# Two pools in the Mamba stage, group-norm scales made inside the attention loop, and a different order of key loads

## The chip, the cores and the metric

The kernel runs on one core of one Trainium2 chip. The metric is device time in microseconds. Before the change three runs took 4524.57, 4528.81 and 4533.37 us; their median is 4528.81 us. One further execution was profiled; its trace is the source of all timelines and rows below.

The engines are named as in the profile: PE (TensorE; PEld is its weight load), DVE (VectorE), ACT (ScalarE), POOL (GpSimd) and SP (SyncE, which issues DMAs). A queue name with a "q" (SPq) marks an instruction that issues a DMA or waits.

## The reference

Two layers, each with a group norm ahead and a residual sum behind it, on two images of 256 channels and 64 x 64 = 4096 pixels, in float32:

```
x = x + mamba_block(gn(x))        # layer norm, W_in, conv4, silu, selective scan over 4096 steps,
                                  # gate silu(z), W_out, + yn, then an MLP of 256-1024-256 with exact gelu
qkv = qkv_w @ gn(x) + qkv_b       # 8 heads of 32 channels
x = x + softmax(q^T k / sqrt(32)) @ v
gn(v): 32 groups of 8 channels, (v - mean) / sqrt(var + 1e-5)
```

## The kernel before

**Mamba stage.** `mamba_stage` walks 16 tiles of 512 columns, eight for each image. Its work is written as tasks with a cost and a due time, and `Plan.order` sorts them into one list which fixes the order of instructions on each engine. All its SBUF tiles come out of pools: weights from `l0w`, and the working tiles, as rings (`Ring`), from the pool `l0s` (`sb`): `u`, `z`, `xm`, `dt`, `b`, `c`, `h` and others of the scan, and `yn`, `hid`, `x_back` of the part behind it. A tile's tail is: output projection (L625, reads `z`), the MLP up with gelu (L429 `w`, L650 writes `hid`), the MLP down (L661), the sum (L671), the group-norm statistics (L672 into `stats1`), the store to `x_dram` (L675). The image is kept in `Scratch` in DRAM.

The Mamba stage also makes q, k and v of image 0 (`qkv`, one call per tile): the tile's x is loaded back into a `hid` tile, normalised, projected, split into a high and a low half (L714 on ACT, L718 on DVE) and stored to `qk_dram` (L723) and `v_dram`. Since `hid` is a ring of one, the last gelus have to wait for the last of these stores to land.

**Attention.** `attention_block` runs once for each image. It opens its pools in this order: `wp` (`v`, `b_qkv`, `ones`), PSUM pools, `p2` (queries, 2 buffers), `kp` (keys, 8), `ep` and `ec` (exponentials). Memory is handed out by pool, so a pool of the attention can be written only when what lay at its addresses in the stage before has been read.

For image 0 (`prepared`), `load_prepared` loads the queries of the first tile, then eight times a tile of keys and of values, all on SP. For image 1, `prepare` makes q, k and v itself: it loads `w_qkv`, makes the group-norm scales from the statistics (`group_norm_scales`, L30), and for eight tiles loads x (L984), normalises (L988), projects k and q (L998), splits and stores them (L1008 to L1011), projects v (L1021) and copies it from PSUM to SBUF (L1028, DVE). Behind each tile's projections it loads the keys of the tile before it. All of it is under `manual_schedule`, so each engine gets its instructions in the order of the code.

The loop then has 512 steps for an image (2 groups of heads x 8 query tiles x 32 key chunks). Step s does two exponentials of 128 x 1024 on ACT (L1108), the product with v for step s-1 on PE (L1129), and the logits of step s+1 on PE (four matmuls, L1095) into two of three PSUM buffers `s`. DVE and POOL sum the exponentials (L1121, L1157 to L1162). The end of a query tile (`finish`) is a generator, run a piece at a time by `Slots`: each `yield n` puts the next piece n steps later; it is started by `side.start(slot, generator)`, and `side.run()` is called once a step, between `values` and `logits`.

The scales before the change end in a square root on ACT and a reciprocal on DVE:

```
nc.scalar.activation(sd, ps2[:, 0:1], AF.Sqrt, bias=eps_t)
nc.vector.reciprocal(sc[:, 1:2], sd)
```

Of the kernel before, what the change touches and what calls it, by code (L numbers as in the profile page):

```python
# [26 lines left out]
EPS = 1e-5  # L27


def group_norm_scales(nc, small, psum, tag, stats, gmat, eps_t):  # L30


    out = []
    for k in range(stats.shape[1]):
        mv = small.tile([P, 2], F32, name="gn_mv")
        nc.vector.bn_aggr(mv, stats[:, k, :, :].rearrange("p a s -> p (a s)"))
        ps = psum.tile([P, T], F32, name="gn_mean_ps", tag=tag)
        nc.tensor.matmul(ps[:, 0:1], lhsT=gmat, rhs=mv[:, 0:1], start=True, stop=True)
        sc = small.tile([P, 2], F32, name="gn_sc", bufs=4)
        nc.vector.tensor_copy(sc[:, 0:1], ps[:, 0:1])  # L40


        d = small.tile([P, 1], F32, name="gn_d")
        nc.vector.tensor_sub(d, mv[:, 0:1], sc[:, 0:1])
        e = small.tile([P, 1], F32, name="gn_e")
        nc.vector.scalar_tensor_tensor(e, d, d, mv[:, 1:2], ALU.mult, ALU.add)
        ps2 = psum.tile([P, T], F32, name="gn_var_ps", tag=tag)
        nc.tensor.matmul(ps2[:, 0:1], lhsT=gmat, rhs=e, start=True, stop=True)
        sd = small.tile([P, 1], F32, name="gn_sd")
        nc.scalar.activation(sd, ps2[:, 0:1], AF.Sqrt, bias=eps_t)  # L50
        nc.vector.reciprocal(sc[:, 1:2], sd)
        out.append(sc)
    return out


class Slots:
# [196 lines left out]
def mamba_stage(ctx, tc, xs, stats_out, consts, w, outs, scratch):  # L253
# [43 lines left out]
    r_yn, r_u, r_z = ring("yn", 3, KC), ring("u", KD + 1), ring("z", KD)  # L297
    r_xm = Ring(sb, [P, HALO + T], "xm", 3)
    r_tmp = ring("tmp", 3, free=True)
    r_lw, r_dt = ring("lw", 2), ring("dt", 2)  # L300
    r_dtr, r_dtur = ring("dt_rep", 4, 2), ring("dtu_rep", 4, 2)
    r_b, r_c = ring("b", NQ), ring("c", NQ)
    r_da0, r_da1 = ring("da0", 3), ring("da1", 2, pool=ps)
    r_bn, r_dbu1 = ring("bn", 2, pool=ps), ring("dbu1", 3)
    r_h, r_y = ring("h", 5, 2), ring("y", 1, pool=ps)
    r_proj, r_bc = ring("proj", 2), ring("bc", 1, rows=NP)
    r_hid, r_xb = ring("hid", 1, KH), ring("x_back", 1, KC)
    r_gn = Ring(sb, [P, 8], "gn", 2)

# [595 lines left out]
        return self.x[b * KG : (b + 1) * KG].rearrange("g c t -> (g c) t")  # L905


def load_stack(nc, dst, src, which):

    src = src.rearrange("s c h t -> s c (h t)")
    dst = dst.rearrange("p h t -> p (h t)").bitcast(F32)
    for i in range(2):
        if which:
            nc.sync.dma_start(dst[2 * i * D : 2 * (i + 1) * D, :], src.rearrange("s c x -> (s c) x"))
        else:
            for j in range(2):
                nc.sync.dma_start(dst[(2 * i + j) * D : (2 * i + j + 1) * D, :], src[i])


@with_exitstack
def attention_block(ctx, tc, b, stats, consts, w, out, scratch, range_t, prepared):

# [26 lines left out]
    p2 = ctx.enter_context(tc.tile_pool(name=f"l1p2{b}", bufs=2))  # L951
# [6 lines left out]
    def load_keys(g, t):  # L958


        k = keys[g, t] = (kq if g and t == 0 else kp).tile([P, 4, T], F32R, name="k")
        load_stack(nc, k, scratch.qk[b * KG + g, 1, t], 1)

    def load_queries(i):
        if i < KG * NT:
            g, t = divmod(i, NT)
            q = queries[i] = p2.tile([P, 4, T], F32R, name="q")
            load_stack(nc, q, scratch.qk[b * KG + g, 0, t], 0)

    def s_tile():  # L970
        return ps_s.tile([P, 2, T], F32, name="s", tag="s")

    def prepare():

        with tc.tile_pool(name=f"l1p{b}", bufs=2) as pp:
            w_qkv = pp.tile([P, KC, 3 * C], F32, name="w_qkv", bufs=1)
            nc.sync.dma_start(w_qkv, w["qkv_wT"].rearrange("(k p) f -> p k f", p=P))
# [38 lines left out]
            def project_values(t):  # L1016
                pm = s_tile()
                flat = pm.rearrange("p a t -> p (a t)")
                for j in range(T // P):
                    for c in range(KC):  # L1020
                        nc.tensor.matmul(  # L1021
                            flat[:, bass.ts(j, C)],
                            lhsT=xn[t][:, c, bass.ts(j, P)],
                            rhs=w_qkv[:, c, 2 * C : 3 * C],
                            start=(c == 0),
                            stop=(c == KC - 1),
                        )
                nc.vector.tensor_copy(v[:, bass.ts(t, T // P), :].rearrange("p s c -> p (s c)"), flat)  # L1028

            with tc.manual_schedule():  # L1030
                load_x(0)
                load_x(1)
                normalise(0)
                for t in range(NT):
                    project(t, 1)
                    if t + 1 < NT:
                        normalise(t + 1)
                    project(t, 0)
                    project_values(t)
                    load_x(t + 2)  # L1040

                    if t == 1:
                        load_queries(0)
                    if t > 0:
                        load_keys(0, t - 1)
                load_keys(0, NT - 1)

    def load_prepared():
        def load_values(g, t):
            cs = bass.ts(t, T // P)  # L1050
            nc.sync.dma_start(v[:, cs, g * P : (g + 1) * P], scratch.v[b * KG + g, :, cs, :])
# [112 lines left out]
    def finish(i):  # L1164
# [31 lines left out]
        nc.vector.scalar_tensor_tensor(res, po, bias, res, ALU.add, ALU.add)  # L1196
        nc.sync.dma_start(out[g * P : (g + 1) * P, cols], res)

    with tc.manual_schedule():
        logits(0, 0)  # L1200
        logits(0, 1)
        s = 0
        while s <= S or side.waiting:
            i, c = divmod(s, NC)
            if s < S:
                if c == 0:
                    tiles[i] = Slot()
                    load_queries(i + 1)
                if i % NT == NT - 1 and i < KG * NT - 1 and c % (T // P) == 0:
# [12 lines left out]
            logits(s + 1, 1)  # L1222
            if s < S:
                add_up(s)
            s += 1
# [25 lines left out]
def attention_any_range(ctx, tc, consts, w, out, scratch):  # L1251
# [20 lines left out]
    with tc.For_i(0, groups, 1) as g:  # L1272
        k = p1.tile([P, NT, 4, T], F32R, name="g_k")
        for t in range(NT):
            load_stack(nc, k[:, t], scratch.qk[bass.ds(g, 1), 1, t].rearrange("o s c h t -> (o s) c h t"), 1)
        v = p1.tile([P, NC, P], F32, name="g_v")
        nc.sync.dma_start(v, scratch.v[bass.ds(g, 1)].rearrange("o p s c -> (o p) s c"))
        bias = p1.tile([P, 1], F32, name="g_bias")
        nc.vector.tensor_copy(bias, bv.rearrange("p b g -> p (b g)")[:, bass.ds(g, 1)])
        with tc.For_i(0, NT, 1) as t:  # L1280
            q = p1.tile([P, 4, T], F32R, name="g_q")
            load_stack(nc, q, scratch.qk[bass.ds(g, 1), 0, bass.ds(t, 1)].rearrange("o n s c h t -> (o n s) c h t"), 0)
# [43 lines left out]
def conv_preact_kernel(ctx: ExitStack, tc: tile.TileContext, x: bass.AP, w: dict, out: bass.AP):  # L1326
# [20 lines left out]
    for b in range(B):  # L1347
        attention_block(tc, b, stats1[b], consts, w, out[b], scratch, range_t, b == 0)
# [54 lines left out]
```

## Time and profile before

| | us |
|---|---|
| median of three runs | 4528.81 |
| the profiled execution | 4520.82 |
| its span | 4519.0 |
| PE busy | 4247.1 (94%) |
| DVE busy | 3926.9 (87%) |
| POOL busy | 3818.5 (84%) |
| ACT busy | 3755.4 (83%) |
| mean rate of DMA | 86 GB/s |

The page cuts the span into 40 slices of 113 us. In a row of slices each digit is the busy share in tenths; PEclk is the clock granted to PE, in tenths of full speed. Slices 0 to 18 are the Mamba stage, 19 to 28 the attention of image 0, 29 to 39 that of image 1. In a timeline a line has the start, the time it covers, the engine, the source line, the operation with its output and inputs, how many were grouped, and in brackets the idle time before it and what ended that. A DMA's line gives the time of its issue; when it lands is told by a separate answer of the trace. In a group of instructions the columns are busy time and mean ns of one.

### The profile page before, as it was taken

What the parts mean: (1) busy time and instruction counts of PE and PEld (TensorE: products, weight loads), DVE (VectorE), ACT (ScalarE), POOL (GpSimd) and SP (SyncE); (2) the same over time, 40 slices, a digit from 0 to 9 for tenths busy, and PEclk for the clock granted to TensorE, in tenths of its full rate; (3) what the DMA queues carried; (4) which work ended last, traced back from release to release, by engine and by line L of the source; (5) the groups of instructions that cost most, each with busy time, mean ns of one, the idle gap of its engine ahead of it and who ended that gap; (6) DMA issues with size and microseconds to landing.
All of it is one profiled execution on the core that took longest, in us unless ns stands there. A gap on an engine that the chain in (4) does not pass through costs nothing. (4 is left out here: it accounts for less than half of the span.)

```text
span 4519.0 us, 53949 instructions
## 1 busy us (share of the span) xinstructions
PE 4247.1 (94%) x18530; PEld 1639.2 (36%) x18530; DVE 3926.9 (87%) x3316; ACT 3755.4 (83%) x4830; POOL 3818.5 (84%) x2251
## 2 busy tenths in 40 slices
PE   5789999999999999997999999999899999999998
PEld 2233333333333333333333333333343333333333
DVE  4999999999999989993888989889848898898988
ACT  4788888888788888873999999999739999999997
POOL 2999999999999999993888888888608888888887
PEclk8899999999999999998999999999999999999999
DMA  5233333333444434444311040110091110401100
GB/s 192 94 121 103 109 123 121 127 126 127 143 159 131 142 123 138 140 149 116 78 27 29 17 101 17 26 29 20 24 269 35 45 27 18 101 17 26 29 20 8
DMA packets 173066, 389.24 MB, mean 86 GB/s; under 512 B 24176, under 2 KB 50544, under 8 KB 164592
## 3 DMA queue, kind: packets, MB, share of 16 engines
q1 hardware_dynamic: 172784, 385.73, 28.0%
q8 instruction: 147, 2.41, 0.2%
q14 instruction: 135, 1.11, 0.1%
HBM read 292.34 MB, written 93.32 MB: 85 GB/s over the span
## 5 line engine op out<-in xcount | busy, mean ns | idle before, releaser
L1121 DVE TENSOR_REDUCE chunk<-chunk 128x1024 f32<-128x4096 f32 x288 | 1269.8, 4409 | 227.3 <-ACT chunk L1108 203.9
L1108 ACT ACTIVATE chunk<-s 128x1024 f32<-128x1024 f32 x992 | 1118.2, 1127 | 178.5 <-PE s L1095 139.9
L1162 POOL TENSOR_TENSOR acc_p<-acc_p,e 128x1024 f32<-128x1024 f32 x480 | 1152.1, 2400 | 134.8 <-ACT e L1108 116.0
L1095 PE MATMUL s<-q,k 128*128 128x512 f32 x4096 | 1225.6, 421 | 17.8 <-DMA v<-v_dram 15.2
L829 POOL TENSOR_TENSOR h<-h,c 128x1024 f32<-128x1024 f32 x512 | 1206.7, 2368 | 40.4 <-ACT state L826 29.4
L1129 PE MATMUL po<-chunk,v 128*32 128x512 f32 x3968 | 1114.6, 640 | 0.0
L1129 PE MATMUL po<-e,v 128*32 128x512 f32 x4224 | 1079.0, 605 | 0.0
L1108 ACT ACTIVATE e<-s 128x1024 f32<-128x1024 f32 x1056 | 1070.3, 1017 | 7.6 <-PE s L1095 7.2
L1095 PEld LDWEIGHTS s<-q,k 128*128 128x128 f32 x4096 | 689.8, 188 | 1021.8 <-issue 926.8
L812 ACT ACTIVATE da<-dt_rep,neg_a 128x512 f32<-128x512 f32 x1024 | 690.8, 701 | 133.5 <-DVE h L823 107.3
L1160 POOL TENSOR_TENSOR acc_p<-acc_p,e 128x512 f32<-128x512 f32 x480 | 630.6, 1314 | 162.2 <-ACT e L1108 139.4
L823 DVE TENSOR_TENSOR_SCAN h<-da,state,dbu 128x512 f32<-128x512 f32 x512 | 650.4, 1273 | 43.2 <-POOL dbu L818 39.9
L823 DVE TENSOR_TENSOR_SCAN h<-da,state,bn 128x512 f32<-128x512 f32 x512 | 646.9, 1264 | 11.6
L818 POOL TENSOR_TENSOR dbu<-dtu_rep,b 128x512 f32<-128x512 f32 x384 | 487.6, 1281 | 17.7 <-DMA dtu_rep<-dtu_dram 13.1
L238 ACT ACT_TABLE_LOAD x332 | 426.0, 1283 | 6.6 <-PEq L1393 0.7
L429 PE MATMUL bn<-proj,pick 112*128 112x512 f32 x512 | 297.5, 597 | 112.0 <-DVE h L823 111.3
L855 PE MATMUL y<-h,sum 128*32 128x512 f32 x2048 | 357.0, 634 | 36.9 <-POOL h L829 36.5
L818 DVE TENSOR_TENSOR bn<-dtu_rep,bn 128x512 f32<-128x512 f32 x512 | 348.5, 681 | 39.5 <-PE bn L429 23.0
L1159 DVE TENSOR_TENSOR acc<-acc,e 128x512 f32<-128x512 f32 x448 | 309.7, 691 | 24.3 <-ACT e L1108 13.8
L1129 PEld LDWEIGHTS po<-chunk,v 128*32 128x32 f32 x3968 | 142.9, 108 | 360.7 <-issue 349.6
L429 PE MATMUL mm<-yn,w_in 128*128 128x512 f32 x512 | 253.6, 622 | 12.4 <-ACT yn L518 11.2
L429 PE MATMUL mm<-yn,w 128*128 128x512 f32 x512 | 243.9, 606 | 3.2 <-ACT u L562 1.4
(135 smaller groups left out, 4054.0 us busy)
## 6 DMA issues: line engine op xcount, KB each, us to landing
dt_rep<-dt_dram SPq DMA_DIRECT2D x128, 512.0 KB, 4.9
dtu_rep<-dtu_dram SPq DMA_DIRECT2D x128, 512.0 KB, 5.6
q<-qk_dram SPq DMA_DIRECT2D x128, 256.0 KB, 4.8
k<-qk_dram SPq DMA_DIRECT2D x64, 512.0 KB, 8.2
b<-bc_dram SPq DMA_DIRECT2D x64, 256.0 KB, 3.0
c<-bc_dram SPq DMA_DIRECT2D x64, 256.0 KB, 3.7
dt_dram<-dt SPq DMA_DIRECT2D x64, 256.0 KB, 2.0
dtu_dram<-lw SPq DMA_DIRECT2D x64, 256.0 KB, 2.4
```

Of the source, the lines that this page charges most:

```text
L238: self.nc.scalar.preload_act_table_set(self.TABLES[task.table])
L429: nc.tensor.matmul(out, lhsT=lhsT, rhs=rhs, start=(i == 0), stop=(i == len(pairs) - 1))
L812: nc.scalar.activation(da[j].tile, dt.tile[:, j, :], AF.Exp, scale=scale)
L818: engine.tensor_mul(out.tile, dtu.tile[:, j, :], rows.tile)
L823: nc.vector.tensor_tensor_scan(h.tile[:, j, :], da[j].tile, dbu.tile, initial, ALU.mult, ALU.add)
L829: nc.gpsimd.tensor_tensor(h.tile, h.tile, rows_c.tile.unsqueeze(1).to_broadcast([P, 2, T]), ALU.mult)
L1095: nc.tensor.matmul(ps[:, j, :], lhsT=keys[i // NT, kt][:, h, kj : kj + P], rhs=queries[i][:, h, :], start=True, stop=True)
L1108: nc.scalar.activation(e, todo[s].s[half], AF.Exp, scale=SCALE)
L1121: nc.vector.tensor_reduce(out, terms, AX.XY, ALU.add)
L1129: nc.tensor.matmul(tiles[i].po[h * D : (h + 1) * D, :], lhsT=v[:, c, g * P + h * D : g * P + (h + 1) * D], rhs=todo[s].e[h // 2][:, h % 2, :],
L1160: nc.gpsimd.tensor_add(acc_p[:, 1, :], acc_p[:, 1, :], eb[:, 1, :])
L1162: nc.gpsimd.tensor_add(acc_p, acc_p, eb)
```

## The change

- In the Mamba stage the scan's rings (`u`, `z`, `xm`, `tmp`, `lw`, `dt`, `dt_rep`, `dtu_rep`, `b`, `c`, `da0`, `dbu1`, `h`, `bc`) come from a new pool `l0r`, opened first. `yn`, `hid`, `x_back`, `proj` and `gn` stay in `l0s`. The order of the Mamba stage's own instructions is the same on every engine.
- In `attention_block` the pool of the queries is opened first.
- `load_prepared` issues the first queries, the first keys and the first values from ACT; the others stay on SP. In the built program these and the load of `w_next` are placed among the last instructions of the Mamba stage. On SP, `b_qkv`, `w_next` (768 KB) and one of four pieces of the second tile's queries (256 KB) stand ahead of the last L723 store; on ACT the first queries stand between the last L714 and the gelus.
- The weights of image 1's projections (`w_next`) are loaded at image 0's start into a pool `next` that lives through both calls.
- `group_norm_scales` is now a generator. It runs in image 0's loop from slot 34: first two `bn_aggr` (DVE), three slots later two matmuls into an `s` buffer and six small DVE operations, three slots later two matmuls into an `s` buffer and, on ACT, Ln and Exp with a scale of -0.5 for each of the two halves of the channels. Ln and Exp are in different table sets as the program is built: ACT gets four table loads here, before each of the four activations.
- Image 1's `prepare` keeps its projections, without load and scales. V is copied on ACT. The keys of tiles 0, 1 and 2 are loaded behind tiles 1, 2 and 3, and the other five behind all projections.
- The exp table, which was loaded at the end of image 1's projections, is not loaded there any more.

```diff
-def group_norm_scales(nc, small, psum, tag, stats, gmat, eps_t):
...
+def group_norm_scales(nc, small, psum_tile, stats, gmat, eps_t, out):
...
+    for k in range(KC):
+        nc.vector.bn_aggr(mv[k], stats[:, k, :, :].rearrange("p a s -> p (a s)"))
+    yield 3
+    ps = psum_tile()
+    for k in range(KC):
+        nc.tensor.matmul(ps[:, 0, k : k + 1], lhsT=gmat, rhs=mv[k][:, 0:1], start=True, stop=True)
+    for k in range(KC):
+        nc.vector.tensor_copy(out[k][:, 0:1], ps[:, 0, k : k + 1])
...
+    for k in range(KC):
+        nc.vector.tensor_sub(e[k][:, 0:1], mv[k][:, 0:1], out[k][:, 0:1])
+        nc.vector.scalar_tensor_tensor(e[k][:, 1:2], e[k][:, 0:1], e[k][:, 0:1], mv[k][:, 1:2], ALU.mult, ALU.add)
+    yield 3
+    ps = psum_tile()
+    for k in range(KC):
+        nc.tensor.matmul(ps[:, 0, k : k + 1], lhsT=gmat, rhs=e[k][:, 1:2], start=True, stop=True)
+    for k in range(KC):
+        nc.scalar.activation(e[k][:, 0:1], ps[:, 0, k : k + 1], AF.Ln, bias=eps_t)
+        nc.scalar.activation(out[k][:, 1:2], e[k][:, 0:1], AF.Exp, scale=-0.5)
...
+    sc = ctx.enter_context(tc.tile_pool(name="l0r", bufs=2))
     wp = ctx.enter_context(tc.tile_pool(name="l0w", bufs=1))
     sb = ctx.enter_context(tc.tile_pool(name="l0s", bufs=2))
...
+    r_u, r_z = ring("u", KD + 1, pool=sc), ring("z", KD, pool=sc)
...
+    p2 = ctx.enter_context(tc.tile_pool(name=f"l1p2{b}", bufs=2))
     wp = ctx.enter_context(tc.tile_pool(name=f"l1w{b}", bufs=1))
...
+        w_qkv, gn = ahead
         with tc.tile_pool(name=f"l1p{b}", bufs=2) as pp:
-            w_qkv = pp.tile([P, KC, 3 * C], F32, name="w_qkv", bufs=1)
-            nc.sync.dma_start(w_qkv, w["qkv_wT"].rearrange("(k p) f -> p k f", p=P))
-            gn = group_norm_scales(nc, pp, ps_s, "s", stats, gmat, eps_t)
...
-                nc.vector.tensor_copy(v[:, bass.ts(t, T // P), :].rearrange("p s c -> p (s c)"), flat)
+                nc.scalar.copy(v[:, bass.ts(t, T // P), :].rearrange("p s c -> p (s c)"), flat)
...
-                    if t > 0:
+                    if 0 < t <= FIRST:
                         load_keys(0, t - 1)
-                load_keys(0, NT - 1)
+                for t in range(FIRST, NT):
+                    load_keys(0, t)
...
-            load_queries(0)
-            for t in range(NT):
+            load_queries(0, nc.scalar)
+            load_keys(0, 0, nc.scalar)
+            load_values(0, 0, nc.scalar)
+            for t in range(1, NT):
                 load_keys(0, t)
                 load_values(0, t)
...
+    if prepared:
+        w_next, gn_next, stats_next, small = ahead
+        nc.sync.dma_start(w_next, w["qkv_wT"].rearrange("(k p) f -> p k f", p=P))
+
+        side.start(NC + 2, group_norm_scales(nc, small, s_tile, stats_next, gmat, eps_t, gn_next))
```

FIRST is 3.

More of the change, by code (lines that the diff above doesn't have):

```diff
@@ L27 @@
 EPS = 1e-5
-def group_norm_scales(nc, small, psum, tag, stats, gmat, eps_t):
[L33 to L53, printed above, removed]
+def group_norm_scales(nc, small, psum_tile, stats, gmat, eps_t, out):
+    KC = stats.shape[1]
+    mv = [small.tile([P, 2], F32, name=f"gn_mv{k}") for k in range(KC)]
+    e = [small.tile([P, 2], F32, name=f"gn_e{k}") for k in range(KC)]
+    out += [small.tile([P, 2], F32, name=f"gn_sc{k}") for k in range(KC)]
+    for k in range(KC):
[16 more added lines that the diff above has]
+        nc.scalar.activation(out[k][:, 1:2], e[k][:, 0:1], AF.Exp, scale=-0.5)
 class Slots:
@@ L296, in mamba_stage @@
     mm = ring("mm", 3, pool=ps, free=True)
[L297 to L306, printed above, removed]
+    r_yn = ring("yn", 3, KC)
+    r_u, r_z = ring("u", KD + 1, pool=sc), ring("z", KD, pool=sc)
+    r_xm = Ring(sc, [P, HALO + T], "xm", 3)
+    r_tmp = ring("tmp", 3, pool=sc, free=True)
+    r_lw, r_dt = ring("lw", 2, pool=sc), ring("dt", 2, pool=sc)
+    r_dtr, r_dtur = ring("dt_rep", 4, 2, pool=sc), ring("dtu_rep", 4, 2, pool=sc)
+    r_b, r_c = ring("b", NQ, pool=sc), ring("c", NQ, pool=sc)
+    r_da0, r_da1 = ring("da0", 3, pool=sc), ring("da1", 2, pool=ps)
+    r_bn, r_dbu1 = ring("bn", 2, pool=ps), ring("dbu1", 3, pool=sc)
+    r_h, r_y = ring("h", 5, 2, pool=sc), ring("y", 1, pool=ps)
+    r_proj, r_bc = ring("proj", 2), ring("bc", 1, rows=NP, pool=sc)
     r_hid, r_xb = ring("hid", 1, KH), ring("x_back", 1, KC)
@@ L905, in image, with load_stack @@
         return self.x[b * KG : (b + 1) * KG].rearrange("g c t -> (g c) t")
-def load_stack(nc, dst, src, which):
+def load_stack(queue, dst, src, which):
     src = src.rearrange("s c h t -> s c (h t)")
@@ L915, in load_stack, with attention_block @@
         if which:
-            nc.sync.dma_start(dst[2 * i * D : 2 * (i + 1) * D, :], src.rearrange("s c x -> (s c) x"))
+            queue.dma_start(dst[2 * i * D : 2 * (i + 1) * D, :], src.rearrange("s c x -> (s c) x"))
         else:
             for j in range(2):
-                nc.sync.dma_start(dst[(2 * i + j) * D : (2 * i + j + 1) * D, :], src[i])
+                queue.dma_start(dst[(2 * i + j) * D : (2 * i + j + 1) * D, :], src[i])
 @with_exitstack
-def attention_block(ctx, tc, b, stats, consts, w, out, scratch, range_t, prepared):
+def attention_block(ctx, tc, b, stats, consts, w, out, scratch, range_t, prepared, ahead):
     nc = tc.nc
@@ L950, in attention_block @@
     v = wp.tile([P, NC, C], F32, name="v")
-    p2 = ctx.enter_context(tc.tile_pool(name=f"l1p2{b}", bufs=2))
     kp = ctx.enter_context(tc.tile_pool(name=f"l1k{b}", bufs=NT))
@@ L956, in attention_block, with load_keys, load_queries @@
     queries = {}
-    def load_keys(g, t):
+    def load_keys(g, t, queue=nc.sync):
         k = keys[g, t] = (kq if g and t == 0 else kp).tile([P, 4, T], F32R, name="k")
-        load_stack(nc, k, scratch.qk[b * KG + g, 1, t], 1)
-    def load_queries(i):
+        load_stack(queue, k, scratch.qk[b * KG + g, 1, t], 1)
+    def load_queries(i, queue=nc.sync):
         if i < KG * NT:
@@ L967, in load_queries @@
             q = queries[i] = p2.tile([P, 4, T], F32R, name="q")
-            load_stack(nc, q, scratch.qk[b * KG + g, 0, t], 0)
+            load_stack(queue, q, scratch.qk[b * KG + g, 0, t], 0)
     def s_tile():
         return ps_s.tile([P, 2, T], F32, name="s", tag="s")
+    FIRST = 3
     def prepare():
+        w_qkv, gn = ahead
         with tc.tile_pool(name=f"l1p{b}", bufs=2) as pp:
-            w_qkv = pp.tile([P, KC, 3 * C], F32, name="w_qkv", bufs=1)
-            nc.sync.dma_start(w_qkv, w["qkv_wT"].rearrange("(k p) f -> p k f", p=P))
-            gn = group_norm_scales(nc, pp, ps_s, "s", stats, gmat, eps_t)
             xn = {}
@@ L1043, in prepare, with load_values @@
                         load_queries(0)
-                    if t > 0:
+                    if 0 < t <= FIRST:
                         load_keys(0, t - 1)
-                load_keys(0, NT - 1)
+                for t in range(FIRST, NT):
+                    load_keys(0, t)
     def load_prepared():
-        def load_values(g, t):
+        def load_values(g, t, queue=nc.sync):
             cs = bass.ts(t, T // P)
-            nc.sync.dma_start(v[:, cs, g * P : (g + 1) * P], scratch.v[b * KG + g, :, cs, :])
+            queue.dma_start(v[:, cs, g * P : (g + 1) * P], scratch.v[b * KG + g, :, cs, :])
         with tc.manual_schedule():
-            load_queries(0)
-            for t in range(NT):
+            load_queries(0, nc.scalar)
+            load_keys(0, 0, nc.scalar)
+            load_values(0, 0, nc.scalar)
+            for t in range(1, NT):
                 load_keys(0, t)
@@ L1274, in attention_any_range @@
         for t in range(NT):
-            load_stack(nc, k[:, t], scratch.qk[bass.ds(g, 1), 1, t].rearrange("o s c h t -> (o s) c h t"), 1)
+            load_stack(nc.sync, k[:, t], scratch.qk[bass.ds(g, 1), 1, t].rearrange("o s c h t -> (o s) c h t"), 1)
         v = p1.tile([P, NC, P], F32, name="g_v")
@@ L1281, in attention_any_range @@
             q = p1.tile([P, 4, T], F32R, name="g_q")
-            load_stack(nc, q, scratch.qk[bass.ds(g, 1), 0, bass.ds(t, 1)].rearrange("o n s c h t -> (o n s) c h t"), 0)
+            load_stack(nc.sync, q, scratch.qk[bass.ds(g, 1), 0, bass.ds(t, 1)].rearrange("o n s c h t -> (o n s) c h t"), 0)
             o = p1.tile([P, T], F32, name="g_o")
@@ L1346, in conv_preact_kernel @@
     mamba_stage(tc, [x[b] for b in range(B)], stats1, consts, w, [scratch.image(b) for b in range(B)], scratch)
-    for b in range(B):
-        attention_block(tc, b, stats1[b], consts, w, out[b], scratch, range_t, b == 0)
+    with tc.tile_pool(name="next", bufs=1) as pool:
+        w_qkv = pool.tile([P, KC, 3 * C], F32, name="w_next")
+        gn = []
+        attention_block(tc, 0, stats1[0], consts, w, out[0], scratch, range_t, True, (w_qkv, gn, stats1[1], pool))
+        attention_block(tc, 1, stats1[1], consts, w, out[1], scratch, range_t, False, (w_qkv, gn))
     flag = out_of_range(tc, range_t)
```

## The prediction

> **What bounds the kernel now.** I first read the page's rows of 40 slices, to see which engine fills which stage.
>
> ```profile
> PE   5789999999999999997999999999899999999998
> PEclk8899999999999999998999999999999999999999
> DMA  5233333333444434444311040110091110401100
> ```
>
> TensorE (PE) is full everywhere but at the start, in slice 19 (2034 to 2147 us, Mamba stage to attention of image 0) and in slices 29 and 30 (image 0 to image 1). The change works there, and in one place of a stage where PE is full. The windows say how full (columns: us, busy time of the five engines, granted clock, DMA share, GB/s):
>
> ```profile
> 2300.00:3200.00 900.00, 900.00 (x5006) 343.38 (x5004) 803.38 (x458) 824.90 (x818) 756.84 (x408) 1.00 0.13 32
> 2112.00:2122.80 10.80, 0.02 (x1) 0.05 (x1) 0.00 (x0) 0.00 (x0) 0.00 (x0) 0.50 1.03 217
> ```
>
> In the loop PE has no free time and ScalarE (ACT) 8% of it; in the first transition nothing works for 10.8 us but the DMA engines, at 217 GB/s. The timeline there (start, us, engine, line; in brackets the idle time before it and its releaser):
>
> ```profile
> 2075.22 4.76 SPq L723 DMA_DIRECT2D qk_dram<-hid  x2
> ...
> 2082.56 1.84 ACT L650 ACTIVATE hid<-mm,b 128x512 f32<-128x512 f32 x3 [2.47 <-DMA qk_dram<-hid]
> 2083.30 8.85 PE L429 MATMUL mm<-yn,w 128*128 128x512 f32 x20 [1.04 <-ACT hid L650]
> ...
> 2109.35 2.41 SPq L919 DMA_DIRECT2D q<-qk_dram  x4
> 2111.93 1.17 SPq L916 DMA_DIRECT2D k<-qk_dram  x2
> 2122.78 2.90 PE L1095 MATMUL s<-q,k 128*128 128x512 f32 x6 [15.18 <-DMA v<-v_dram]
> 2124.12 1.28 ACT L1108 ACT_TABLE_LOAD   x1 [31.25 <-PE s L1095]
> 2125.41 1.07 ACT L1108 ACTIVATE chunk<-s 128x1024 f32<-128x1024 f32 x1
> ```
>
> The Mamba stage's last matmul ends at 2107.60, the loads of queries and keys start only then, and the first exp comes at 2125.41. Also: the last L723 store (issued 2079.60, landing 2082.4) already holds up the last gelus (L650 overwrites `hid`), and PE through them by 1.04. The second transition:
>
> ```profile
> 3265.41 0.34 SPq L1197 DMA_DIRECT2D out<-res  x1
> 3267.74 0.38 SPq L977 DMA_DIRECT2D w_qkv<-in_qkv_wT  x1
> 3268.17 1.49 SPq L984 DMA_DIRECT2D xn<-x_dram  x2
> 3270.22 1.28 ACT L50 ACT_TABLE_LOAD   x1 [18.11 <-PE gn_var_ps L48]
> 3273.60 1.00 DVE L988 TENSOR_SCALAR xn<-xn,gn_sc 128x512 f32<-128x512 f32 x2 [1.23 <-DMA xn<-x_dram]
> 3274.20 0.50 PEld L998 LDWEIGHTS s<-xn,w_qkv 128*128 128x128 f32 x2 [2.42 <-DVE xn L988]
> ```
>
> The wait that ends last there is that of xn's load; the scales were ready at 3272.36.
>
> **1. First transition: saves about 10.0 us.** The scan's buffers lie in their own pool, so image 0's queries, keys and values may be loaded once `z` is read (L625, 2075.4), 30 us before the tail's end. Queries and the first keys will be there. What is left between the last matmul (2107.60) and the first exp: the last L671 ends 2108.39, logits run meanwhile if a PSUM buffer is free, the exp waits for the table (1.28) behind whatever tail it waits for: 2108.45 + 0.9 + 1.29, or 2110.6 against 2125.41, a gain of 14.8.
>
> Against it stands what moves ahead of the last L723 store. On SP's queue now come `b_qkv`, the load of `w_next` (768 KB) and a quarter of the second queries (256 KB) before it, and on ACT's queue image 0's queries run beside it. At 217 GB/s, 1 MB is 4.8 us; `w_qkv`, the same load alone, took 4.4. These loads can start about 3 us before the store, so it lands between 0.8 and 4.1 us later than 2082.4; I take 2.4, the middle. The gelus wait for it, and behind them on ACT the issue of the keys, on PE all of the MLP's second half. PE's pause grows from 1.04 to 3.4 us, and that has a second price:
>
> ```profile
> 3320.30:3327.10 6.80, 4.63 (x6) 2.05 (x7) 3.54 (x5) 0.69 (x1) 0.00 (x0) 0.50 0.98 303
> 3327.10:3332.00 4.90, 4.90 (x14) 2.24 (x13) 1.50 (x2) 1.39 (x3) 0.00 (x0) 1.00 1.11 320
> ```
>
> Here PE had paused 4.18 us for a late xn; the clock was at 0.50 for a while, and the 16 matmuls took 9.43 instead of 7.03: 2.4 us more. So T1 = 14.8 - 2.4 - 2.4 = 10.0, with ends 14.0 (store 0.8 late, no clock loss) and 5.5 (4.1, plus the clock, plus some lateness of keys).
>
> Here a rule speaks against the change. The Trainium skill, "DMA: Bandwidth & Descriptors", section "Issuing engines are not separate DMA queues", says that transfers issued from several engines share the same 16 DMA engines, so that a second issuer saves issue time only. If the ACT loads were free, the store would be late by SP's own 1 MB alone (0.8 to 1.8); by the rule, everything in flight counts and it goes to 4.1. The trace of before shows one issuer only here, so it can't say; I take a value between.
>
> **2. Second transition: saves about 4.9 us.** Gone are the `w_qkv` load ahead of the two xn loads and the chain of scales. Xn still waits for the last output's landing (3267.54). Alone, a load of 512 KB lands after 3.7 us (row of `hid<-x_dram`); behind `w_qkv` these took 5.3 and 6.3. From 3267.74, not 3268.17, the xn is there at 3271.5 instead of 3273.5: 2.05 earlier. The scales' chain hid behind that load with 1.1 us to spare (3272.36 against 3273.50); left in place it would now end last and take 0.9 back, which is all that its removal is worth here. Next late is the stall at the fourth tile:
>
> ```profile
> 3322.47 9.43 PE L998 MATMUL s<-xn,w_qkv 128*128 128x512 f32 x16 [4.18 <-DVE xn L988]
> 3347.35 7.13 PE L998 MATMUL s<-xn,w_qkv 128*128 128x512 f32 x16 [1.67 <-DVE xn L988]
> 3359.77 7.13 PE L998 MATMUL s<-xn,w_qkv 128*128 128x512 f32 x16 [1.83 <-DVE xn L988]
> ```
>
> Keys 0 to 2 are still loaded in front of xn of tiles 4 to 6, so the stalls of 4.18 and 1.67 stay; in front of tile 7 there are no keys any more: 1.83 + 0.1 goes, 2.0 in all, partly given back if the query pieces land there. The copy of v goes from VectorE to ACT, which is idle most of this stage (11.0 of 50 us busy at 3300), and takes at worst the place of a `halves` activation (687 ns). At the end the late halves (3371.80 after logits at 3370.00) may come earlier by 0.75, and the exp table, loaded at 3369.40 behind the last halves, is already there. Keys 3 to 7, 5 MB, come in 24 us at 217 GB/s, and key 3 is wanted 12 steps of 2.18 us after the first: in time, just. Sum 2.05 + 2.0 + 0.75 = 4.8, with the table 4.9; ends 3.5 and 6.5 (the query pieces stall tile 7 after all; the fourth tile is helped too).
>
> **3. The scales in the loop: cost about 8.4 us.** At slot 40 ACT loads a table four times and does two Ln and two Exp of one column:
>
> ```profile
> L238 ACT ACT_TABLE_LOAD x332 | 426.0, 1283 | 6.6 <-PEq L1393 0.7
> ...
> 2213.78 1.03 ACT L1108 ACTIVATE e<-s 128x1024 f32<-128x1024 f32 x1
> 2214.96 1.13 ACT L1108 ACTIVATE chunk<-s 128x1024 f32<-128x1024 f32 x1 [0.15 <-PE s L1095]
> ```
>
> 4 x 1.283 + 4 x 0.262 (the row of L50's Sqrt) = 6.2 us. `e` ends at 2214.81; the next chunk starts at 2221.0 instead of 2214.96, its `e` ends 2223.2, and values (L1129), which begin at 2217.50 now, begin at about 2223.35: PE loses 5.85, and with three `s` buffers it can't run ahead of that. Slot 37's two matmuls and six small VectorE operations hold an `s` buffer for some 1.0 us (L38 to L48 took 1.3 per half), worth 0.6; behind the reduce (L1121, 4.42 at 2209.59) they would hold it, and the logits queued behind on PE, for up to 4 more, but VectorE idles 1.65 just ahead of it. The two L36 of slot 34 (0.38 each) lie in VectorE's free time (803 of 900 us). PE pauses twice (about 3.2 and 2.1 us) and here too comes a slow clock:
>
> ```profile
> 1982.30:1985.70 3.40, 3.40 (x9) 0.68 (x10) 3.40 (x5) 3.35 (x6) 3.40 (x3) 0.50 0.83 308
> ```
>
> That window followed a pause of 1.9 us: 3.4 us at half clock lose 1.7. One to two such windows: 2.0. Sum 5.85 + 0.6 + 2.0, or 8.4; ends 6.0 (no clock loss, slot 37 free) and 11 (two windows, and slot 37 behind part of a reduce).
>
> A second rule: the Trainium skill, "ScalarE: Activation LUTs", section "What ACT_TABLE_LOAD costs", gives a switch as the load of about 1.28 us and a drain of about 1.38 before it. By the row four switches cost 5.1, by the page 10.6, and the loop would lose 5.5 more, making the change worth 1 us. The row shows no such drain: the load at 3369.40 starts as the last `halves` ends. I take the row.
>
> **Sum.** -10.0 - 4.9 + 8.4 = -6.5 us on the profiled execution of 4520.82 (span 4519.0), which is 8.0 below the median; on the median, 4528.8 - 6.5 = 4522.3, so 4522.
>
> **The rivals.**
> - A, both transitions pay in full: the store lands no more than 0.8 late and PE's clock stays up: -14.0 - 5.5 + 6.0 = -13.5, 4515. For it: the ACT issues are few; against: 1 MB stands in front of the store. Chance 0.32.
> - B, more comes back: the store 4 us late and the drain between table loads shows: -6 - 4.5 + 10 = about -0.5, 4528. Chance 0.14.
> - C, the other side, slower. The store comes to lie among the loads like the keys in a full queue: those took up to 17.9 us to land against 2.8, so 15.1 late, and 2.4 for the clock; T1 is then +2.7 instead of -10 and the total +6.2, 4535. The sum is lateness less 8.9 us: from 8.9 on the whole is a loss, and from 18 on by over 0.2%. For it: ACT's queue too waits behind the gelus; against: only about 1.3 MB can be ahead of it. Chance 0.07.
> - D, the change doesn't do it: keys are early, but xn is as late as now in the second image: -10 - 2 + 8.4 = -3.6, 4525. Inside the main case's range.
>
> **How the numbers follow.** 0.2% is 9 us, about what a measurement of this kernel can tell from no change. Main case (with D) 0.47, from -3 to -12 (4517 to 4526), a third of it beyond -9. Faster: 0.32 + 0.17 = 0.49 or so; slower: half of C and a little of B, 0.06; the rest the same, 0.45. The range leaves the far ends of A and C out: 4510 to 4532.
>
> **What would show it.** First transition: first exp near 2115, a gap before it below 5 us, L723's landing at 2084 to 2086, PE's pause before L650's release about 3 us. Loop: one ACT stretch of 6.2 us with four table loads near the 40th step, no 11 us. Second: first L998 about 2 us sooner after the output's landing, the stall of 4.18 still there, that of tile 7 gone. Wrong would be: keys or values late after the first step, table loads with drains, xn waiting for something else than the output.

## The result, and the profile after

The changed kernel takes 4518.06 us (median of 20 runs, 4511.53 to 4523.67), the kernel before 4524.35 beside it (20 runs, 4516.6 to 4533.37). The ratio is 0.9987, with a 95% interval of 0.9981 to 0.9993: 5.9 us less by the ratio, between 3 and 9. The prediction said 6.5 less. The total came out right, in part by luck: two of its three terms were off by 2 to 4 us, a loss of 2 us was not in the sum at all, and these errors cancel. The profiled execution of the changed kernel has a span of 4520.6 us, more than the 4519.0 of before, because its Mamba stage was 7.9 us longer in that execution; so the two profiles must be compared stage by stage.

Two of the rows of 40 slices of the changed kernel:

```profile
PE   5789999999999999988999999999899999999998
...
DMA  5233333333443434446110040100081110401100
```

Counted from 0, the 7 of PE in slice 18 (the prediction, which counts from 1, calls it 19) has become an 8, with another 8 in slice 17, and DMA work of slice 19 moved into slice 18. The next view is the first transition of the changed kernel, in its timeline. L731, L658 and L1122 are here what L723, L650 and L1108 were before. The first of the two last lines is the store at 2088.59 with its size and the us from its issue to its landing, the second the same store before the change.

```profile
2083.40 0.41 ACTq L927 DMA_DIRECT2D q<-qk_dram  x1
...
2084.07 1.19 SPq L1215 DMA_DIRECT2D w_next<-in_qkv_wT  x1
...
2088.59 0.38 SPq L731 DMA_DIRECT2D qk_dram<-hid  x1
...
2095.53 0.69 ACT L658 ACTIVATE hid<-mm,b 128x512 f32<-128x512 f32 x1 [6.44 <-DMA qk_dram<-hid]
...
2096.27 10.92 PE L437 MATMUL mm<-yn,w 128*128 128x512 f32 x20 [5.66 <-ACT hid L658]
...
2123.49 1.67 PE L1109 MATMUL s<-q,k 128*128 128x512 f32 x6 [0.84 <-DVE x_back L679]
2124.29 1.28 ACT L1122 ACT_TABLE_LOAD   x1 [16.37 <-PE s L1109]
2125.58 1.07 ACT L1122 ACTIVATE chunk<-s 128x1024 f32<-128x1024 f32 x1
...
qk_dram<-hid SPq DMA_DIRECT2D x1, 512.0 KB, 6.8
...
qk_dram<-hid SPq DMA_DIRECT2D x1, 512.0 KB, 2.8
```

The 15.18 us of waiting for loads are gone. The last store of k, q halves now lands 6.8 us after its issue (2.8 before), so the gelus come late, PE pauses 5.66 us, and its 20 matmuls take 10.92 instead of 8.85. The clock right behind that pause, in the windows (us, busy time of PE, PEld, DVE, ACT, POOL, granted clock, DMA share, GB/s):

```profile
2096.20:2099.60 3.40, 3.33 (x4) 1.51 (x5) 0.00 (x0) 1.17 (x3) 0.00 (x0) 0.50 1.03 217
```

The place in the loop where the scales are made, ACT and PE only:

```profile
2214.48 1.04 ACT L1122 ACTIVATE e<-s 128x1024 f32<-128x1024 f32 x1
...
2215.53 1.28 ACT L56 ACT_TABLE_LOAD   x1
...
2216.83 0.26 ACT L56 ACTIVATE gn_e<-s,eps_t 128x1 f32<-128x1 f32 x1
...
2217.11 1.28 ACT L57 ACT_TABLE_LOAD   x1
...
2220.20 1.28 ACT L57 ACT_TABLE_LOAD   x1
2220.23 1.22 PE L1109 MATMUL s<-q,k 128*128 128x512 f32 x2 [2.63 <-ACT gn_e L56]
2221.49 0.20 ACT L57 ACTIVATE gn_sc<-gn_e 128x1 f32<-128x1 f32 x1
2221.60 1.05 ACT L1122 ACTIVATE chunk<-s 128x1024 f32<-128x1024 f32 x1
```

Four loads and four small activations fill ACT from 2215.53 to 2221.69, 6.16 us; between an activation and the next load, and between a load and its activation, there are at most 0.02 us and no drain. And the second transition, in which the eight tiles of image 1 are counted from 0 (the line at 3326.80 is tile 4, the "fourth tile" of the prediction):

```profile
3273.98 0.34 SPq L1211 DMA_DIRECT2D out<-res  x1
...
3276.21 0.89 SPq L994 DMA_DIRECT2D xn<-x_dram  x2
...
3280.67 9.20 PE L1008 MATMUL s<-xn,w_next 128*128 128x512 f32 x16 [13.65 <-DVE xn L998]
...
3326.80 7.13 PE L1008 MATMUL s<-xn,w_next 128*128 128x512 f32 x16 [2.51 <-DVE xn L998]
...
3339.49 8.83 PE L1008 MATMUL s<-xn,w_next 128*128 128x512 f32 x16 [2.10 <-DVE xn L998]
...
3351.60 7.03 PE L1008 MATMUL s<-xn,w_next 128*128 128x512 f32 x16
...
3361.92 7.03 PE L1008 MATMUL s<-xn,w_next 128*128 128x512 f32 x16
```

From the issue of the output to the first projection it is 6.69 us; before it was 8.79. Tiles 6 and 7 (3351.60, 3361.92) start without a pause.

By stage, from the starts and ends of single instructions in the profiled executions (the second profile of before is an experiment below):

| us | before | before, again | after |
|---|---|---|---|
| start of the span to the end of the last output projection | 2075.39 | 2081.24 | 2083.32 |
| from there to the first exponential | 50.02 | 49.89 | 42.26 |
| steps 30 to 60 of image 0 | 66.15 | 66.15 | 73.61 |
| one query tile of 32 steps, mean of 13 | 70.513 | 70.513 | 70.580 |
| start of the last exponential of image 0 to step 10 of image 1 | 142.61 | 140.51 | 134.94 |
| from there to the end | 1125.35 | 1125.93 | 1125.98 |

### The profile page after: what moved, and what is told of

Same layout as the page of the kernel before. It is cut to its first block, busy times and chain, and to the rows that moved or that the text cites. A ratio compares the mean times of both kernels' runs of the same rounds, so it can differ in the third digit from the quotient of the medians.

```text
span 4520.6 us, 53932 instructions
## 1 busy us (share of the span) xinstructions
PE 4252.8 (94%) x18530; PEld 1637.9 (36%) x18530; DVE 3922.2 (87%) x3306; ACT 3766.1 (83%) x4842; POOL 3817.0 (84%) x2251
## 4 chain that ended last, share of the span: by engine, by line
PE 64%; POOL 12%; DVE 9%; issue 6%; ACT 5%; DMA 3%; SPq 0%; POOLq 0%; DVEq 0%; ACTq 0%
PE s L1109 26%; PE po L1143 24%; PE mm L437 8%; POOL h L837 6%; DVE h L831 5%; POOL dbu L826 3%; PE y L863 2%; ACT L242 2%; ACT da L820 1%; DVE bn L826 1%; PE mm L669 1%; PE mm L633 1%; PE s L1008 1%; PE bn L437 1%; DMA dtu_rep<-dtu_dram 1%
## 5 line engine op out<-in xcount | busy, mean ns | idle before, releaser
L1122 ACT ACTIVATE chunk<-s 128x1024 f32<-128x1024 f32 x992 | 1117.1, 1126 | 181.6 <-PE s L1109 140.3
L1122 ACT ACTIVATE e<-s 128x1024 f32<-128x1024 f32 x1056 | 1073.9, 1020 | 7.3 <-PE s L1109 6.6
```

Of the source, the lines that this page charges most:

```text
L1122: nc.scalar.activation(e, todo[s].s[half], AF.Exp, scale=SCALE)
```

## The experiments

Each is an edit of the changed kernel unless said otherwise. "Faster" is against the kernel before, measured beside it. The 95% interval of one such time is 6 to 13 us wide, so a miss of 1 to 3 us in the total says little by itself; what an edit did is read from the stage in its trace.

**The scales back in the transition.** The generator is replaced by the old function (square root and reciprocal), called ahead of the loads of x.

```diff
-        side.start(NC + 2, group_norm_scales(nc, small, s_tile, stats_next, gmat, eps_t, gn_next))
...
         with tc.tile_pool(name=f"l1p{b}", bufs=2) as pp:
+            gn = group_norm_scales(nc, pp, ps_s, "s", stats, gmat, eps_t)
```

> The changed kernel, with image 1's scales made in the transition again (square root and reciprocal, ahead of the loads of x), the weights still loaded early. If the scales in the loop cost what the profile of the changed kernel shows (7.5 us at slots 37 to 41), the loop of image 0 has no break there, and the transition gives back about 1 us, since the chain of scales (4.8 us after the output's landing before) ends later than the load of x (3.7): 12 to 14 us faster than before. If that break only took up time that the loop would have lost anyway, the time stays at 6 us faster than before or gets worse by the 1 us.

4512.14 us against 4522.86, ratio 0.9977 (0.9968 to 0.9986): 10.7 faster, short of the 12 to 14 expected (the interval reaches to 14), and past the 6 of the rival. Steps 30 to 60 take 66.22 again, so the loop's break is all the scales' work. The transition gave back more than the expected 1 us in two places: the first projection starts 0.8 later after the last exponential (21.77 against 21.01), and at its end the exp table, which the square root had displaced, is loaded in the open:

```profile
3359.14 1.01 ACT L1035 COPY v<-s 128x1024 f32<-128x1024 f32 x1 [1.21 <-PE s L1028]
...
3360.17 1.28 ACT L1119 ACT_TABLE_LOAD   x1
...
3361.47 1.07 ACT L1119 ACTIVATE chunk<-s 128x1024 f32<-128x1024 f32 x1
```

From the last projection to step 10 it is 25.15 us, against 22.20 in the changed kernel: the load of 1.28, and behind it a PE pause of 1.64 and a granted clock of 0.82 and 0.67 in two windows of 3.4 us (1.00 in the changed kernel). The transition as a whole took 135.32 in this profile, hardly more than the 134.94 of the changed kernel, because the pauses at tiles 4 and 5 were 3.3 us shorter; these differ from one execution to the next. Before the change the table load was hidden: it ended at 3370.68, and the exponential still waited 0.16 us for PE. With v's copy on ACT it lies behind that copy.

**One table for Ln and Exp.**

```diff
+    nc.scalar.preload_act_table_set("natural_log_exp_and_others")
     for k in range(KC):
         nc.scalar.activation(e[k][:, 0:1], ps[:, 0, k : k + 1], AF.Ln, bias=eps_t)
```

> The changed kernel with one table that holds both Ln and Exp loaded ahead of the four small activations: one table load of 1.28 us in place of four, the scales still in the loop. If ACT's table loads are the price, ACT's stretch falls from 6.2 to 2.3 us, PE's break from 7.5 to between 1.5 and 3 us (the slow clock goes with it): 10 to 12 us faster than before. If the price lies in the matmuls' waits for VectorE and the buffers they hold, nothing changes: 6 us faster than before.

4509.18 us, ratio 0.9969 (0.9958 to 0.9981): 13.7 faster, more than the 10 to 12 expected (the interval begins at 9). Its timeline in the loop:

```profile
2211.86 1.28 ACT L55 ACT_TABLE_LOAD   x1
...
2213.84 0.20 ACT L58 ACTIVATE gn_sc<-gn_e 128x1 f32<-128x1 f32 x1
...
2213.95 1.07 ACT L1123 ACTIVATE chunk<-s 128x1024 f32<-128x1024 f32 x1
```

2.2 us of ACT instead of 6.2; steps 30 to 60 take 68.04, which is 1.9 over before in place of 7.5. That is 5.6 us back for three loads of 1.28; the clock has a part in it. The windows right behind the break, of the changed kernel and then of this one (columns as above):

```profile
2220.20:2223.60 3.40, 2.12 (x4) 1.00 (x4) 1.81 (x3) 3.39 (x5) 0.00 (x0) 0.50 0.00 0
```

```profile
2213.80:2217.20 3.40, 2.94 (x17) 1.13 (x14) 3.40 (x4) 3.37 (x6) 1.41 (x2) 1.00 0.00 0
```

In this profile the second transition took 130.39, 4.5 less than in that of the changed kernel, though the edit does not touch it: it varies by some us from one execution to the next (the pauses of tiles 4 and 5, see below).

**The weights' load behind the store.**

```diff
-        nc.sync.dma_start(w_next, w["qkv_wT"].rearrange("(k p) f -> p k f", p=P))
...
-                    load_queries(i + 1)
+                if c == (8 if prepared and i == 0 else 0):
+                    load_queries(i + 1)
+                if prepared and s == NC // 2:
+                    nc.sync.dma_start(w_next, w["qkv_wT"].rearrange("(k p) f -> p k f", p=P))
```

> The changed kernel with the load of w_next (768 KB) issued behind the last L723 store and the second queries; the rest as it is, the first quarter of the second queries still ahead of the store. If the store is late by what stands ahead of it in the queues, it lands 3.3 to 4.5 us after its issue, not 6.8; PE's pause before the last gelus falls from 5.7 to 2 to 3 us, and the time from that store's issue to the first exp by 3 to 5 us: 9 to 11 us faster than before. If the loads on ACT's queue are what delays it, it still takes 6 us or more, and the time moves by less than 1 us.

4514.96 us, ratio 0.9983 (0.9976 to 0.9989): 7.9 faster, under the 9 to 11 expected (the interval is 5 to 11).

```profile
2088.11 0.69 ACT L658 ACTIVATE hid<-mm,b 128x512 f32<-128x512 f32 x1 [4.70 <-DMA qk_dram<-hid]
...
2088.85 11.34 PE L437 MATMUL mm<-yn,w 128*128 128x512 f32 x20 [3.91 <-ACT hid L658]
```

The store took 5.0 us, not 3.3 to 4.5, and PE still pauses 3.91 and runs slow after it. So the weights account for 1.8 of the 4.1 us by which the store is late; the rest is the queries, those on ACT's queue included. Neither of the two theories alone holds.

**Everything on SP.**

```diff
-            load_queries(0, nc.scalar)
-            load_keys(0, 0, nc.scalar)
-            load_values(0, 0, nc.scalar)
+            load_queries(0)
+            load_keys(0, 0)
+            load_values(0, 0)
```

> The changed kernel with the first queries, keys and values issued from SP like the others. The builder then puts one quarter of the first queries (256 KB) ahead of the last L723 store and all else, w_next at the end, behind it. If bytes in flight are what delays the store, it lands within 3 to 4.5 us, the gelus wait 1 to 2.5 us, and queries and keys still come before the tail ends: 10 to 13 us faster than before. If it is the second issuing engine that brings the keys in time, the first exp comes later than 2.2 us after the last sum of the Mamba stage, by the keys' lateness of 5 us or more, and the time is that of before or worse.

4511.01 us, ratio 0.9974 (0.9966 to 0.9983): 11.9 faster, within 10 to 13.

```profile
2088.23 1.84 ACT L658 ACTIVATE hid<-mm,b 128x512 f32<-128x512 f32 x3 [2.87 <-DMA qk_dram<-hid]
...
2088.97 8.85 PE L437 MATMUL mm<-yn,w 128*128 128x512 f32 x20 [1.55 <-ACT hid L658]
...
2116.21 1.07 ACT L1122 ACTIVATE chunk<-s 128x1024 f32<-128x1024 f32 x1
```

With a quarter of the first queries alone ahead of it the store lands in 3.2 us, PE pauses 1.55, and the 20 matmuls take 8.85 again. From the last output projection to the first exponential it is 35.66 us, 14.4 less than before. Keys and values were in time without ACT's queue.

**One pool.** The pools as before, the loads as in the change.

```diff
-    sc = ctx.enter_context(tc.tile_pool(name="l0r", bufs=2))
...
-    r_u, r_z = ring("u", KD + 1, pool=sc), ring("z", KD, pool=sc)
+    r_u, r_z = ring("u", KD + 1), ring("z", KD)
...
     v = wp.tile([P, NC, C], F32, name="v")
+    p2 = ctx.enter_context(tc.tile_pool(name=f"l1p2{b}", bufs=2))
```

> The changed kernel with all of the Mamba stage's rings in one pool again and the queries' pool in its old place; the loads keep their issuing engines. If the two pools are what lets queries and keys come early, the first exp comes again 15 to 19 us after the stage's last matmul, the last L723 store lands after 2.8 us as before, and the time is 0 to 3 us slower than before (what the loop costs, less what the second transition gains). If the issue from ACT alone were enough, the time is that of the changed kernel.

4535.78 us against 4523.13, ratio 1.0031 (1.0019 to 1.0044): 12.7 slower, more than the 0 to 3 expected.

```profile
2112.24 1.01 SPq L1214 DMA_DIRECT2D w_next<-in_qkv_wT  x1
...
2114.40 3.89 SPq L926 DMA_DIRECT2D q<-qk_dram  x4
...
2121.54 2.70 ACTq L923 DMA_DIRECT2D k<-qk_dram  x2
...
2138.13 3.32 PE L1108 MATMUL s<-q,k 128*128 128x512 f32 x7 [27.65 <-DMA v<-v_dram]
```

The loads start after the tail again, as expected, but PE now waits 27.65 us instead of 15.18: `w_next` and the second queries lie ahead of the first keys. The pools are thus worth 18.8 us to this kernel (61.09 us from the last output projection to the first exponential, against 42.26), because the other edits have put 1.75 MB more in front of the keys (768 KB and 1 MB).

**The keys between the projections again.**

```diff
-    FIRST = 3
+    FIRST = NT - 1
```

> The changed kernel with the keys of every tile but the last loaded behind the next tile's projections again, as before the change. If keys in front of x are what makes tiles 6 and 7 late, their pauses of 1.7 and 1.8 us come back and the second transition (last exponential of image 0 to the 11th step of image 1, 134.9 us in the changed kernel, 142.6 before) gets 3 to 5 us longer: 1 to 3 us faster than before. If the pauses went for another reason (v's copy on ACT, the weights out of the way), the transition stays within 1 us.

4523.87 us against 4523.13, ratio 1.0004 (0.9997 to 1.001): nothing is left of the gain, less than the 1 to 3 us expected. The second transition takes 138.25, in the foreseen band:

```profile
3345.08 7.13 PE L1008 MATMUL s<-xn,w_next 128*128 128x512 f32 x16 [0.92 <-DVE xn L998]
...
3357.18 7.13 PE L1008 MATMUL s<-xn,w_next 128*128 128x512 f32 x16 [1.51 <-DVE xn L998]
```

The pauses of tiles 6 and 7 are back, smaller than before the change (1.67 and 1.83), and the end is longer: from the last projection to step 10 it is 25.96 us (22.20 in the changed kernel), as the last stores of halves queue behind keys and the exponentials behind the halves.

**V's copy on VectorE.**

```diff
-                nc.scalar.copy(v[:, bass.ts(t, T // P), :].rearrange("p s c -> p (s c)"), flat)
+                nc.vector.tensor_copy(v[:, bass.ts(t, T // P), :].rearrange("p s c -> p (s c)"), flat)
```

> The changed kernel with v copied from PSUM by VectorE again. If the copy is hidden on either engine, the second transition stays within 1 us of the changed kernel's 130 to 135. If it is VectorE's time for the copy that delayed the normalised x and the low halves, the stall at the fourth tile goes back from 2.5 towards 4.2 us, with the slow clock behind it, and the transition gets 2 to 4 us longer.

4517.43 us, ratio 0.9988 (0.998 to 0.9997): as the changed kernel. The transition takes 131.61; the copy is hidden on either engine.

**Before, once more.**

> The kernel before, once more. In the profile of the changed kernel the Mamba stage's last output projection ends 7.9 us later than in that of before, ahead of anything that the change touches. If this is the spread from one execution to the next, this run ends it at 2077 to 2083 like the changed ones; if the change causes it (buffers at other addresses), it ends at 2075 again.

Its last output projection ends at 2081.24, in the span of 2076.35 to 2083.32 of the twelve profiles of the changed kernel and its variants (their mean is 2079.9, that of the two profiles of before 2078.3). So the 7.9 us by which the changed kernel's Mamba stage was longer in its profile are mostly the spread between executions; with two profiles of before, a small cost of the new pools in that stage is not ruled out. Its second transition took 140.51 against 142.61, with a pause of 1.90 instead of 4.18 at tile 4: that stall is no fixed quantity either.

**A version with both mends.** Joint table and everything on SP. The edits below it start from this version.

> Both mended parts together: one joint table load in the loop, and the first queries, keys and values issued from SP with w_next behind them. If the stages add up (first transition 35.7 us from the last output projection to the first exponential, steps 30 to 60 in 68.0 us, second transition 130 to 135), it is 18 to 20 us faster than before. If the gains overlap, it is no better than 15.

4504.26 us against 4525.43, ratio 0.9957 (0.9944 to 0.9971): 21.2 faster. The stages do add up: 35.59, 68.03 and 132.14 us.

**And image 1's first x early.** Both tiles go into a query buffer in the last 24 steps of image 0.

```diff
+            if prepared and s == S - 24:
+                q = p2.tile([P, 4, T], F32R, name="q").bitcast(F32)
+                for t in range(2):
+                    xn_next[t] = q[:, 2 * t : 2 * t + 2, :]
+                    nc.sync.dma_start(xn_next[t], ...)
```

> The same, and the first two tiles of x of image 1 loaded during the last tile of image 0's loop, into the query buffer that has no further use there, and normalised by VectorE in the loop. If x's load, which waits for the last output's landing 16.4 us after the last exponential, is all that keeps the projections from starting, they start 7 to 10 us after it instead of 21, and the time is 10 to 13 us better than without: about 30 us faster than before. If the split halves' buffers, which wait for the same landing, stop PE then, 5 to 8 us remain of it.

4507.16 us, ratio 0.9958 (0.9945 to 0.9972): no better than the version without. The transition did get shorter, 126.95, by 5.2 (PE then waits for the halves, below); but the loop got slower all through, 70.767 us for 32 steps. The pool of the queries had to be opened first here, which moved the queries to another address. That led to the last two runs.

**The address of the queries.** The first takes the version with both mends and opens the queries' pool behind v, as before the change; the second takes the one with x early and puts the pool of the weights in front of the queries.

```diff
     v = wp.tile([P, NC, C], F32, name="v")
+    p2 = ctx.enter_context(tc.tile_pool(name=f"l1p2{b}", bufs=2))
```

> Joint table and loads on SP, with the queries' pool opened behind v again as before the change (queries at byte 58368 of a partition, v at 25600; without this edit 25440 and 41984). In every kernel with the queries' pool first, a query tile of 32 steps took 70.580 us in the loop; before, and with one pool, 70.513. If the address of queries or v sets that, it is 70.513 here and the time falls by 2 us, to 23 us under before. If it is the pools of the Mamba stage or anything else of the change, it stays at 70.580. If the queries then come later to memory, the first transition gets longer than 35.6 us.

4502.16 us, ratio 0.9948 (0.9935 to 0.9962); 32 steps take 70.513 and the first transition 35.60.

```diff
-    with tc.tile_pool(name="l1p2", bufs=2) as p2, tc.tile_pool(name="next", bufs=1) as pool:
+    with tc.tile_pool(name="next", bufs=1) as pool, tc.tile_pool(name="l1p2", bufs=2) as p2:
```

> The kernel with image 1's first x loaded and normalised early, with the pool of the weights in front of that of the queries, so that queries lie at byte 25440 again (there 19104, with 70.767 us for 32 steps). If the queries' address sets the step, it is 70.580 again, the loops of the two images lose 6 us less, and the time is 4501 or below. If the early load itself slowed the loop, it stays at 70.767 and 4507.

4498.58 us against 4522.9, ratio 0.9946 (0.9932 to 0.996): 24.3 faster, the lowest median of all, though the times do not tell it from the run above (0.9935 to 0.9962). 32 steps take 70.580, as the address says. Its second transition (L1007, the projections):

```profile
3242.45 7.13 PE L1007 MATMUL s<-q,w_next 128*128 128x512 f32 x16
...
3257.97 0.34 SPq L1207 DMA_DIRECT2D out<-res  x1
...
3258.40 0.39 SPq L957 DMA_DIRECT2D b_qkv<-in_qkv_b  x1
3261.39 0.69 ACT L1017 ACTIVATE halves<-s,b_qkv 128x512 fp32r<-128x512 f32 x1 [19.97 <-issue]
...
3264.42 6.09 PE L1007 MATMUL s<-q,w_next 128*128 128x512 f32 x7 [10.19 <-DVE halves L1018]
```

The projections start right behind image 0's last values, but PE then stands 10.19 us for the halves, which don't start until 3261.39. What they waited for last, by the trace, is the bias `b_qkv`: its load for image 1 goes out behind image 0's last output (3258.40) and lands at 3260.9, where ACT's wait ends; the output itself, for which ACT waited too, had landed 0.8 us sooner. To load the bias earlier would thus gain 0.8 us at most; that was not run. Of a start 18 us earlier, 5 us remain.

## Why the prediction was right, and where its terms were off

**First transition, 10.0 predicted, 7.7 measured.** The gross gain was right: from the end of the Mamba stage's last matmul to the first exponential it was 17.8 us and is 2.9, 14.9 less (14.8 predicted). The term that was mis-sized is the late store. It was taken at 2.4 us, with ends 0.8 and 4.1, plus 2.4 for the clock. Measured: the store before it is 1.1 late already (the queries on ACT's queue go out 0.26 us behind it), the store itself 4.0, and the slow clock costs 2.1: 7.1 in all instead of 4.8. The rule on issuing engines, weighed there, described it rightly: what is in flight from ACT's queue counts too (with one 256 KB load ahead on SP in either run, the store took 5.0 us with queries on ACT's queue and 3.2 without), and the upper end was the place to be. Moving the weights alone gave back 1.8 us, moving the queries, keys and values to SP and the weights to the end gave back all but 0.4 of the store's lateness.

**The scales in the loop, 8.4 predicted, 7.5 measured.** The step of slot 37 is 0.5 longer (0.6 predicted), that of slot 40 5.9 (5.85), and the two behind it 1.0, with the clock at 0.50 (2.0). That is the mechanism as foreseen; only the price of the clock was too high. On the drain at a table load the prediction was right to go by the profile: 6.16 us for four loads and four activations leave no room for the four drains of about 1.38 us that the Trainium skill ("ScalarE: Activation LUTs", "What ACT_TABLE_LOAD costs") adds to a load. The page gives the drain's length and not its place; the prediction puts it ahead of the load, and the trace has room for it on neither side.

**Second transition, 4.9 predicted; 7.7 less in the two profiles.** With the second profile of before (142.61 and 140.51) and the five kernels with this transition unchanged (134.94, 130.39, 132.56, 133.21, 132.14), the means are 141.6 and 132.6: about 9. The start is 2.1 earlier, as predicted (2.05). The first tile is 0.5 quicker, which is within its spread (8.49 to 9.83 us in the five kernels, 9.67 and 9.99 before). The step that failed is "Keys 0 to 2 are still loaded in front of xn of tiles 4 to 6, so the stalls of 4.18 and 1.67 stay". The stall of tile 6 went with that of tile 7, 3.7 us for both in place of 2.0: it counted only the loads ahead of an x, not those issued right behind it. Before, x of tile 6 was issued at 3338.11 and keys at 3338.62, and x landed after 8.6 us; in the changed kernel, with no keys behind it, after 6.7 (the last line):

```profile
3338.11 0.46 SPq L984 DMA_DIRECT2D xn<-x_dram  x1
3338.62 2.82 SPq L916 DMA_DIRECT2D k<-qk_dram  x2
...
DMA to landing us min/median/max: 8.6/8.6/8.6
...
DMA to landing us min/median/max: 6.7/6.7/6.7
```

In the run with the keys between again it landed after 7.8, and the pause was 0.9. Up to the issue of this x, that run and the changed kernel load the same things in the same order; they first differ in the keys right behind it. It brought back about half of the pause; why not all of it is open. At the end of the projections 1.15 was gained, with 0.75 predicted. The stall of tile 4 differs between executions of one kernel by more than between the two kernels (pauses of 4.18 and 1.90 before, 1.42 to 2.82 in the changed kernel and the variants that load x as it does), so no gain or loss is claimed for it. Tile 5 pauses in the changed kernel (2.10) and did not before, but the pause is no new loss: from the start of tile 4 to that of tile 5 it is 12.69 us, and 12.72 and 12.12 before. Tile 5 waits for its own x, which lands 9.0 us after its issue (8.9 before), and the slow clock of tile 4 before the change (9.43 us for its matmuls) only filled that wait. What the pause did cost in this profile is a slow clock in tile 5 itself, 8.83 us for its matmuls; in most of the variants they took 7.13.

**What was missing: 2 us in the loop.** Its step does not keep its length: 70.580 against 70.513 us for a query tile, over 32 tiles 2.1 us. The prediction took the order of the pools for a matter of when memory is free, and said nothing on where the tiles then lie.

Summed by stage: -7.7 + 7.5 - 7.7 to -9 + 2.1, or -6 to -7, with nothing for the Mamba stage, against a measured -6.3 between the medians. Too much was expected of the first transition, and too little of the second, and one loss was not seen. That the total was met within 1 us is luck in so far as these cancel.

Of the rivals, B's first reason (the store about 4 us late) came true, its second (drains) did not; A's came true in part (the second transition paid more than in full). C, with a store 15 us late, was far off, and D did not come: x of image 1 was 2.1 us earlier.

## What to carry to other kernels

A load that is made early is not free because nothing waits for it: ask which store or load issued in the next 5 us has somebody waiting, on any queue, and put it first. Loads right behind a wanted transfer can cost too (6.7 us without, 7.8 and 8.6 with keys behind x). Work hidden in a loop that is full on one engine is paid there (6.2 us of ACT cost 7.5); look at the tables that an activation brings before moving it.

## What the runs showed of the hardware

The time of a step depended on the address of the queries or v in SBUF, and was the same to the nanosecond, as a mean of 13 query tiles, in every execution with the same addresses. Starts of an exponential 13 query tiles apart, before:

```profile
2265.10 1.14 ACT L1108 ACTIVATE chunk<-s 128x1024 f32<-128x1024 f32 x1 [0.18 <-PE s L1095]
...
3181.78 1.14 ACT L1108 ACTIVATE chunk<-s 128x1024 f32<-128x1024 f32 x1 [0.18 <-PE s L1095]
```

and with x early and the queries' pool first:

```profile
2258.08 1.15 ACT L1118 ACTIVATE chunk<-s 128x1024 f32<-128x1024 f32 x1 [0.18 <-PE s L1105]
...
3178.05 1.16 ACT L1118 ACTIVATE chunk<-s 128x1024 f32<-128x1024 f32 x1 [0.18 <-PE s L1105]
```

The first distance is 916.68 us, 70.51 for a tile, the second 919.97, 70.77. Queries at byte 52032 or 58368 of a partition (v at 19264 or 25600) gave 70.513 in four executions (before twice, the one pool, and the last but one run; these addresses are recorded for the last and follow from the tiles' sizes for the others), queries at 25440 (v at 41984) 70.580 in nine kernels, and queries at 19104 with v at the same 41984 gave 70.767. With v at one address, the queries' address made the difference between the last two; of what the loop's matmuls read, nothing else moved. Why an address costs time was not found.
